# Each gather of edges' rows in the routed experts' attention waits for the landing of the last gather but one

## The chip, the cores and the metric

The kernel runs on one core of a Trainium2 chip. A core has five engines that run their own instruction streams side by side: TensorE (PE, matrix products; PEld is its weight load), VectorE (DVE), ScalarE (ACT), GpSimd (POOL) and SyncE (SP), and 16 DMA engines that move data between main memory (HBM) and on-chip memory (SBUF). Engines wait for each other and for DMA by semaphores. The metric is device time in microseconds (us) from start to end of one execution, as the median over several; a profile is one further execution.

## The reference, cut to what matters

The kernel computes eight blocks, one behind the other, on 3125 nodes of 256 features: a graph layer and a feed-forward layer, four times. The change is in the second block, the feed-forward layer of routed experts, whose router is a small graph attention over 32768 edges:

```python
h = (x_flat @ W_gat).reshape(M, HEADS, NUM_EXPERTS)      # 4 heads, 4 experts
src = jnp.concatenate([edge_index[0], loops])            # 32768 edges and a loop for each node
dst = jnp.concatenate([edge_index[1], loops])
a_src = (h * att_src).sum(-1)
a_dst = (h * att_dst).sum(-1)
e = jax.nn.leaky_relu(a_src[src] + a_dst[dst], negative_slope=0.2)
e_max = jax.ops.segment_max(e, dst, num_segments=M)
ee = jnp.exp(e - e_max[dst])
denom = jax.ops.segment_sum(ee, dst, num_segments=M)
alpha = ee / (denom[dst] + 1e-16)
agg = jax.ops.segment_sum(h[src] * alpha[:, :, None], dst, num_segments=M)
...
topk_s, topk_i = jax.lax.top_k(scores, TOP_K)            # 2 of 4, from agg's layer norm
w = jax.nn.softmax(topk_s, axis=-1)
for ei in range(NUM_EXPERTS):
    g = jnp.where(topk_i == ei, w, 0.0).sum(-1)
    hh = jax.nn.gelu(x @ W1[ei] + b1[ei], approximate=False)
    out = out + g[..., None] * (hh @ W2[ei] + b2[ei])
```

The experts' products do not need the attention; only the last sum, where each expert's output is weighted by its gate, needs both.

## The kernel before, in words

The nodes are padded to 3200 = 25 tiles of 128 (`NT` = 25, `P` = 128). An earlier stage has sorted the edges by their destination; `gsorted` in HBM holds their source nodes in that order, and `gstart_i` says for each node where its edges start. The function of this stage is `routed_layer_in_order` (L1204). It goes as follows.

- The router's logits `hg` and the two sides of the attention's score come from PE and DVE. `node` packs, for each node, 4 scores and 16 logits, which makes a row of 20 numbers or 80 bytes. SP writes it to `nodes` in HBM (L1219).
- The gathers, which are what the change is about: for each of 8 groups, POOL issues 32 indirect DMAs (L1230; the instruction itself is in the helper `gather`, L236), each of which fetches 128 rows of `nodes`, one per partition, into a column of `ge`. Behind each group POOL issues a plain DMA that writes `ge` to the table `edges` in HBM (L1232, 320 KB). There are 256 such gathers in all; `ge` has two buffers. Software-issued DMAs share eight semaphores in turn, and so each gather in the built program waits for the semaphore of the one eight before it.
- `routed_experts` (L1192): for each of 4 experts and each of 7 chunks of columns (six of 512 nodes, one of 128), 8 matrix products `l0f_ph` (L1200), 4 Gelus on ACT (L1201, tile `l0f_ht`), 16 products or fewer of L576 in pairs of loops (tile `l0f_po`, inside the helper `project`), and DVE adds the bias while it empties PSUM (L1288, "evacuation"; 13 of them for each expert). Expert 0's outputs stay in SBUF (`l0f_y_first`), the others go to HBM through `l0f_ys` (L1290).
- The attention itself, in `shares`, is called in the last expert's chunks 2 to 6, each time for five tiles of nodes. POOL gathers from `edges` 40 rows for each node (`el`, five gathers of 128 descriptors of 3200 bytes); DVE copies the node's own row in (L1253), adds the destination's score (L1255), takes the leaky ReLU (L1256), the mask, the maximum and the difference (L1257 to L1259); ACT takes the exponential (L1261); DVE sums (L1262), multiplies (L1264) and adds up the messages (L1269 to L1271). I call these steps for one call the attention chain of a chunk. `tc.issue_after` (L1252, L1260) asks that the first DVE part be ordered behind the chunk's second evacuation, and the exponential behind the chunk's last Gelu.
- `router_gates` (L1114; its first step is L1121, tile `ag`) makes gates from the sums, all on DVE and ACT. Then X is updated with the experts' weighted outputs on DVE (L1302, L1310), and the next stage's normalisation gives `xn` (L456), which PE transposes (L465).

The order of instructions on each engine is set by a planner: it simulates the program with costs that it assumes and lists each engine's instructions by due time. An edit that changes a cost or a dependency can so move instructions elsewhere. `tc.add_manual_dep` adds a dependency between two instructions by hand.

Of the kernel before, what the change touches and what calls it, by code (L numbers as in the profile page):

```python
# [209 lines left out]
def body(ctx, tc, A, out, plan):  # L210
    nc = tc.nc
    V, S, G, T = nc.vector, nc.scalar, nc.gpsimd, nc.tensor

    def pool(stack, name, bufs=1, space=None):
        kw = {} if space is None else {"space": space}
        return stack.enter_context(tc.tile_pool(name=name, bufs=bufs, **kw))
# [6 lines left out]
    def load(stack_pool, ap, shape, name, dtype=F32, **kw):  # L223
        t = stack_pool.tile(shape, dtype, name=name, **kw)
        nc.sync.dma_start(t, ap)
        return t
# [6 lines left out]
        return t  # L233

    def gather(dst, table, idx):
        G.indirect_dma_start(out=dst, out_offset=None, in_=table, in_offset=bass.IndirectOffsetOnAxis(ap=idx, axis=0))  # L236

    def scatter(table, idx, src, **kw):
        G.indirect_dma_start(out=table, out_offset=bass.IndirectOffsetOnAxis(ap=idx, axis=0), in_=src, in_offset=None, **kw)  # L239
# [385 lines left out]
    def edge_softmax(st, nt, chunk, W, dst_row, dst_i, dst_f, sc_i, states, score):  # L625
# [8 lines left out]
        for t in range(nt):  # L634
# [6 lines left out]
            one = slice(t, t + 1)  # L641
            row = ep.tile([P, state.shape[1]], F32, name="row", bufs=6)
            gather(row, state[:NP, :], dst_i[:, one])
            s, v = score(ep, t, row[:, SW:])
            mine = rows[:, k * P : (k + 1) * P]
# [66 lines left out]
    def windows_of(wp, ps, groups, places):  # L712
# [4 lines left out]
        for g in groups:  # L717
            n, K = len(g), WKS[g[0]]
            wd = wd_all[:, g[0] : g[0] + n, :K]
            for t in g:  # L720
                gather(wd_all[:, t, :K].rearrange("p k w -> p (k w)"), plan["rec"][:, :], plan["first"][:, t : t + 1])
# [482 lines left out]
    def routed_layer_in_order():  # L1204

        with ExitStack() as st:
# [5 lines left out]
            with ExitStack() as st2:  # L1212
# [5 lines left out]
                nodes = dram.tile([NP, 20], F32, name="nodes")  # L1218
                nc.sync.dma_start(nodes[:, :].rearrange("(t p) w -> p t w", p=P), node)  # L1219
                part = load(ga, gsorted[:, :].rearrange("(p j) o -> p (j o)", p=P), [P, GT], "src_parts", I32)  # L1220
# [3 lines left out]
                nc.sync.dma_start(edges[GE:, :], pad)  # L1224
                by_part = edges[:GE, :].rearrange("(p j) w -> p j w", p=P)
                gx = pool(st2, "gat_e", 2)
                for j0 in range(0, GT, 32):
                    ge = gx.tile([P, 32, 20], F32, name="ge")
                    for j in range(32):
                        gather(ge[:, j, :], nodes[:, :], part[:, j0 + j : j0 + j + 1])  # L1230

                    G.dma_start(by_part[:, j0 : j0 + 32, :], ge)  # L1232

# [159 lines left out]
    if plan:  # L1393
        routed_layer_in_order()
    else:
        routed_layer_by_states()
# [318 lines left out]
    with ExitStack() as st:  # L1715
# [30 lines left out]
        for e in range(8):  # L1746
# [3 lines left out]
            for c, cl in CHUNKS:  # L1750
                src, at = xt, c
                for layer in range(2):
                    dst = wp.tile([P, 2, 512], F32, name=f"l1f_h{layer}")
# [290 lines left out]
    with ExitStack() as st:  # L2044
# [66 lines left out]
        for i in range(2):  # L2111
            idx = {}
# [125 lines left out]
```

## Time and profile before

| | us |
|---|---|
| median of 6 runs | 5787.35 |
| lowest and highest of them | 5781.7, 5794.35 |
| the profiled execution | 5770.04 |
| its span | 5768.2 |

The mean granted PE clock of the profiled execution is 0.84. Over the span, PE is busy 74%, PEld 46%, DVE 40%, ACT 21%, POOL 27%. The gathers of the change (`ge<-nodes,src_parts`) are 256 instructions of 944 ns on average, 241.7 us in all. The matrix products of this stage are 196.6 us (L1200) and 188.6 us (L576).

In the views, a line of a group reads: line, engine, operation, tile written from tiles read, count, busy time, mean of one, idle time of the engine in front of them and what ended most of it. "remote" is a wait whose releaser the profile does not show. "issue" is time in which the engine waited for nothing that the profile shows. A line of the timeline begins with the start and the duration, both in us, and ends with the idle time before it and its releaser.

### The profile page before, as it was taken

The numbers are of one execution on the slowest core, as the hardware profiler recorded it, in microseconds if no ns is written. First come the engines' busy times: TensorE is split into PE (matmuls) and PEld (weight loads), VectorE is DVE, ScalarE is ACT, GpSimd is POOL, SyncE is SP. The second block draws the span as 40 slices with busy tenths as digits, with TensorE's granted clock in tenths as the row PEclk, the third lists the DMA queues.
The fourth block names the chain that finished last, engine by engine and source line by source line (L and its number), as shares of the span: only waits on it lengthen the run. The fifth ranks groups of instructions, "written<-read, shape, count | busy, mean of one in ns | idle before, by whom it ended". The sixth has DMA issues, their size and how long they took to land. (4 is left out here: it accounts for less than half of the span.)

```text
span 5768.2 us, 56008 instructions
## 1 busy us (share of the span) xinstructions
PE 4263.1 (74%) x20805; PEld 2625.9 (46%) x20889; DVE 2314.3 (40%) x6281; ACT 1186.2 (21%) x2820; POOL 1533.4 (27%) x1496
## 2 busy tenths in 40 slices
PE   2467778215956996666668767788999999797987
PEld 2344444103634664445447433445444445463455
DVE  8765342000075233556555656665101102324042
ACT  0245530001221221333331211222101100120011
POOL 2145440762010002555550356541000000220010
PEclk6667779657978997777878888889999999898999
DMA  1034562001133335554551222210222132224300
GB/s 49 15 127 151 170 202 85 15 14 51 47 128 111 128 128 163 151 153 141 154 151 62 96 92 95 82 50 29 71 77 83 62 96 88 81 81 179 134 24 23
DMA packets 286839, 553.51 MB, mean 96 GB/s; under 512 B 81979, under 2 KB 195148, under 8 KB 275676
## 3 DMA queue, kind: packets, MB, share of 16 engines
q1 hardware_dynamic: 215804, 411.42, 21.1%
q0 software_dynamic: 70752, 138.40, 8.8%
q8 instruction: 167, 2.74, 0.2%
q14 instruction: 116, 0.95, 0.1%
HBM read 377.47 MB, written 172.20 MB: 95 GB/s over the span
## 5 line engine op out<-in xcount | busy, mean ns | idle before, releaser
L558 PE MATMUL agg_ps<-tt,h_l 128*128 128x512 bf16 (+3 forms) x3796 | 882.4, 393 | 54.3 <-ACT h_l L2018 43.8
L236 POOL DMA_INDIRECT h_kv<-kv_tab,kv_row x416 | 435.8, 1048 | 878.9 <-ACT h_odt L1615 562.0
L239 POOL DMA_INDIRECT wgt_cells<-cw_wsum,cw_to x391 | 386.4, 988 | 346.7 <-DVE cw_to L1108 201.0
L558 PEld LDWEIGHTS <-h_l 128*128 128x128 bf16 x3150 | 291.2, 98 | 330.9 <-issue 15.6
L239 POOL DMA_INDIRECT gsorted<-gs_i,gpos x256 | 304.2, 1188 | 434.4 <-DVE gpos L909 321.0
L1200 PE MATMUL l0f_ph<-xt,l0f_w 128*128 128x512 f32 (+1 forms) x448 | 196.6, 583 | 257.0 <-issue 162.4
L1628 PE MATMUL h_pq<-h_q,h_odt 128*128 128x256 bf16 x1248 | 224.4, 351 | 133.3 <-DVE h_qk L1630 100.0
L236 POOL DMA_INDIRECT ge<-nodes,src_parts x256 | 241.7, 944 | 253.7 <-PE l0f_po L576 160.2
L1757 PE MATMUL l1f_ph<-l1f_h,l1f_W 128*128 128x512 f32 (+1 forms) x448 | 226.1, 637 | 96.8 <-ACT l1f_h L1760 83.4
L1760 ACT ACTIVATE l1f_h<-l1f_ph,bn_shift,bn_scale 128x512 f32<-128x512 f32 (+1 forms) x224 | 162.4, 731 | 629.4 <-PE l1f_ph L1757 322.1
L576 PE MATMUL l1f_po<-l1f_Wo,l1f_h 128*128 128x256 f32 x800 | 225.7, 415 | 79.2 <-issue 34.8
L1815 DVE TENSOR_TENSOR at<-agg_ps,rdeg_r 128x512 f32<-128x512 f32 (+1 forms) x42 | 25.6, 633 | 586.3 <-PE agg_ps L558 586.3
L1628 PEld LDWEIGHTS <-h_odt 128*128 128x128 bf16 x1248 | 150.9, 125 | 224.9 <-issue 178.4
L1935 POOL IOTA trash_slot<- 128x32 f32 x1 | 0.2, 158 | 948.2 <-PE l2g_ph L1834 948.2
L1200 PEld LDWEIGHTS l0f_ph<-xt,l0f_w 128*128 128x128 f32 x448 | 84.4, 199 | 352.6 <-issue 248.7
L576 PEld LDWEIGHTS l1f_po<-l1f_Wo,l1f_h 128*128 128x128 f32 x800 | 155.4, 203 | 176.5 <-issue 78.2
L1681 PE MATMUL h_po<-h_kv,h_of 128*128 128x256 f32 x832 | 217.7, 427 | 21.4 <-DVE h_kv L1677 21.4
L576 PE MATMUL l0f_po<-l0f_w,l0f_ht 128*128 128x256 f32 x800 | 188.6, 393 | 39.1 <-ACT l0f_ht L1201 22.3
L558 PEld LDWEIGHTS agg_ps<-tt,h_l 128*128 128x128 f32 x700 | 126.3, 192 | 189.3 <-issue 188.6
L1757 PE MATMUL l1f_ph<-xt,l1f_W 128*128 128x512 f32 (+1 forms) x448 | 207.1, 586 | 1.1 <-issue 1.1
L1681 PEld LDWEIGHTS h_po<-h_kv,h_of 128*128 128x128 f32 x832 | 179.8, 219 | 52.5 <-DVE h_kv L1677 22.6
L465 PE MATMUL pt<-ident,xn 128*128 128x128 f32 x300 | 64.7, 376 | 180.4 <-DVE xn L456 135.5
(625 smaller groups left out, 7575.0 us busy)
## 6 DMA issues: line engine op xcount, KB each, us to landing
tt<-cnt_ds SPq DMA_DIRECT2D x90, 640.0 KB
kv_tab<-kv SPq DMA_DIRECT2D x50, 1024.0 KB
tt<-wgt_cells SPq DMA_DIRECT2D x30, 1280.0 KB
wgt_cells<-cw_zero SPq DMA_DIRECT2D x6, 5800.0 KB
cw_row<-cell_r SPq DMA_DIRECT2D x23, 1128.0 KB
cw_ew<-in_ew_r_dram SPq DMA_DIRECT2D x22, 1108.0 KB
cnt_ds<-row_ds SPq DMA_DIRECT2D x150, 128.0 KB
cnt_sd<-cols SPq DMA_DIRECT2D x6, 3200.0 KB
```

The costliest lines, as they stand in the source:

```text
L236: G.indirect_dma_start(out=dst, out_offset=None, in_=table, in_offset=bass.IndirectOffsetOnAxis(ap=idx, axis=0))
L239: G.indirect_dma_start(out=table, out_offset=bass.IndirectOffsetOnAxis(ap=idx, axis=0), in_=src, in_offset=None, **kw)
L465: T.transpose(pt[:, j, :], src[:, g + j, h * P : (h + 1) * P], ident)
L558: T.matmul(acc[h][:, :width], part[:, s, h * P : (h + 1) * P], tt[:, s - s0, :width], start=(s == 0 and i == 0), stop=(s == NT - 1 and i = ...
L576: T.matmul(psum, lhs[:, i, t * P : (t + 1) * P], rhs[:, i, :], start=(i == 0), stop=(bias is None and i == k - 1))
L1200: T.matmul(ph[:, :cl], w1[:, k, f * P : (f + 1) * P], xt[:, k, c : c + cl], start=(k == 0), stop=(k == 1))
L1628: T.matmul(pq[:, i, :], odt[:, k0 + i, :], q3[:, j, :], start=(j == 0), stop=(j == 2))
L1681: T.matmul(po, of[:, j, :], kv[:, j, D:], start=(k0 + j == 0), stop=(k0 + j == K - 1))
L1757: T.matmul(ph[:, :cl], ws[layer][:, k, o * P : (o + 1) * P], src[:, k, at : at + cl], start=(k == 0), stop=(k == 1))
L1760: S.activation(dst[:, o, :cl], ph[:, :cl], AF.Relu, bias=shi[:, col], scale=sca[:, col])
L1815: V.tensor_tensor(at[:, hf, c : c + cl], psum, rdeg_r[:, c : c + cl], op=OP.mult)
L1935: G.iota(trash, pattern=[[P, 32]], base=NP, channel_multiplier=1, allow_small_or_imprecise_dtypes=True)
```

## The change

`gather` returns its instruction. The loop over the 256 gathers collects them, and each one from the third on gets a dependency on the gather two before it, so that it waits on that gather's semaphore, that is until its 128 rows have landed.

```diff
     def gather(dst, table, idx):
-        G.indirect_dma_start(out=dst, out_offset=None, in_=table, in_offset=bass.IndirectOffsetOnAxis(ap=idx, axis=0))
+        return G.indirect_dma_start(out=dst, out_offset=None, in_=table, in_offset=bass.IndirectOffsetOnAxis(ap=idx, axis=0))
...
                 gx = pool(st2, "gat_e", 2)
+                got = []
                 for j0 in range(0, GT, 32):
                     ge = gx.tile([P, 32, 20], F32, name="ge")
                     for j in range(32):
-                        gather(ge[:, j, :], nodes[:, :], part[:, j0 + j : j0 + j + 1])
+                        got.append(gather(ge[:, j, :], nodes[:, :], part[:, j0 + j : j0 + j + 1]).ins)
+
+                        if len(got) > 2:
+                            tc.add_manual_dep(
+                                got[-1], got[-3].name, mybir.DependencyInfo(mybir.DependencyClass.Sync, mybir.DependencyReason.DATA), reason="rows landed"
+                            )
 
                     G.dma_start(by_part[:, j0 : j0 + 32, :], ge)
```

Lines behind the edges write have numbers six higher in the changed file than before.

## The prediction

> **What bounds the kernel now.** The chain that ended last covers only the end of the program (from 4061 us on) and does not reach this stage, so the place of the change is read from busy time by stretch of the stage, then from the waits in it, then from POOL's own instructions.
>
> Busy time in seven stretches (start:end, length, then PE, PEld, DVE, ACT, POOL busy with counts, granted clock, DMA share, GB/s):
>
> ```profile
> 860.00:1000.00 140.00, 119.44 (x574) 62.39 (x580) 41.84 (x130) 11.53 (x20) 0.23 (x1) 0.93 0.32 94
> 1000.00:1150.00 150.00, 46.33 (x129) 27.01 (x127) 2.77 (x4) 5.50 (x8) 113.97 (x122) 0.63 0.10 15
> 1150.00:1344.00 194.00, 24.07 (x48) 12.05 (x48) 2.77 (x4) 2.75 (x4) 132.17 (x142) 0.54 0.09 16
> 1344.00:1500.00 156.00, 136.40 (x474) 90.83 (x475) 13.04 (x20) 27.67 (x44) 9.45 (x10) 0.90 0.18 63
> 1500.00:1614.00 114.00, 113.93 (x409) 76.33 (x408) 11.45 (x18) 23.45 (x36) 0.00 (x0) 1.00 0.10 39
> 1614.00:1661.00 47.00, 45.00 (x167) 30.02 (x166) 44.53 (x41) 19.85 (x25) 10.68 (x10) 1.00 0.37 121
> 1661.00:1774.00 113.00, 0.27 (x2) 0.22 (x2) 103.50 (x236) 7.64 (x9) 4.75 (x5) 0.52 0.49 163
> ```
>
> While POOL issues the 256 gathers (999.8 to 1338.4) nothing else is busy: PE 70 us of 344, ACT 8, DVE 6, DMA engines 10%. Afterwards PE is full (113.93 of 114) with the other experts, and from 1661 to 1774 it stands still behind DVE. Expert 0 takes 990.5 to 1399, some 407 us; experts 1 to 3 take 262 together, 87.2 each. The waits between 990 and 1700 (engine, line, releaser: us, times, longest):
>
> ```profile
> ACT l0f_ht L1201 <- remote: 331.2, 10, 100.2
> POOL el L236 <- DVE gat_num L1271: 299.2, 3, 278.1
> DVE l0f_y_first L1288 <- issue: 195.1, 4, 88.9
> PE l0f_ph L1200 <- issue: 162.4, 14, 76.8
> ```
>
> The expert loop reads nothing of a gather: its waits in the program are on PE, ACT and DVE. Yet a Gelu waits up to 100 us with no releaser on the page, and its releases lie 10 to 11 us apart or multiples of that. I call this the clog. It begins some 12 gathers after the first and ends by 1373, about 17 us after the last of the ten `el` gathers that follow. POOL in the same time, forms and then its last steps:
>
> ```profile
> L236 POOL DMA_INDIRECT ge<-nodes,src_parts x256: 938/944/988, 999.8 to 1338.4; - x128
> L1232 POOL DMA_DIRECT2D edges<-ge x8: 578/591/604, 1044.5 to 1341.3; - x8
> ```
> ```profile
> 1338.41 0.94 POOL L236 DMA_INDIRECT ge<-nodes,src_parts  x1 [1.16 <-issue]
> 1341.31 0.58 POOL L1232 DMA_DIRECT2D edges<-ge  x1 [1.95 <-DMA ge<-nodes,src_parts]
> 1344.03 0.97 POOL L236 DMA_INDIRECT el<-edges,gstart_i  x1 [2.15 <-DMA edges<-ge]
> ```
>
> A gather is 0.944 us with 0.30 behind it: 1.25 from start to start as far as about 1214, 1.40 after that, 338.6/255 = 1.33 on average. The recorded landings are 2.0 to 2.45 us after a gather's start, all the way.
>
> How the stage ends:
>
> ```profile
> 1613.59 0.69 DVE L1288 TENSOR_TENSOR l0f_ys<-l0f_po,l0f_b 128x512 f32<-128x512 f32 x1 [2.76 <-PE l0f_po L576]
> 1614.48 1.01 DVE L1255 TENSOR_TENSOR gat_s<-el,side_L_ffn_att_dst 128x820 f32<-128x820 f32 x1
> 1700.09 0.58 DVE L1121 TENSOR_TENSOR ag<-gat_num,den 128x400 f32<-128x400 f32 x1
> 1773.73 2.10 PE L465 MATMUL pt<-ident,xn 128*128 128x128 f32 x8 [112.98 <-DVE xn L456]
> ```
>
> The attention chain starts right behind evacuation 6 of expert 3 (1613.59), ends with the gates' first step at 1700.09, and PE's next stage waits for DVE until 1773.73. So the stage is gathers, then experts, then DVE's chain.
>
> **The change part by part.**
>
> *The waits.* Gather n waits for the landing of n-2 in place of n-8 (254 of the 256 get the wait). No instruction is added. Two starts lie 2.50 us apart; the landing is there after 2.0 to 2.45, and POOL starts some 0.25 after a landing (edges landed 2.47 after 1341.31, `el` started at 1344.03). That makes 2.25 to 2.70 for two gathers: 1.25 (the floor of 0.944 + 0.30) to 1.35 each. The dearest row is the last gather to its edges write, 1341.31 - 1338.41 = 2.90: 1.45 each. Against 1.33 now: 255 x (1.45 - 1.33) = +31 at most, 255 x (1.25 - 1.33) = -20 at least. I take +8, near 1.36: the landings are the nearest row, the 2.90 is of the clogged end.
>
> Under "Anatomy of one DMA — SWDGE (gpsimd) path", the Trainium skill's page "DMA: Bandwidth & Descriptors" puts a transfer at 2.0 us plus bytes over 436e3: an estimate of 2.02 for 10 KB. By it the wait never binds and this term is nothing; the row of 2.90 would make it +31.
>
> *What queues behind the waits.* On POOL the eight edges writes, then `el`. The first edges write comes after 33 gathers in the built program (36 before), so it waits for a gather just issued: 2.90 - 1.33 = 1.6 us for each of eight, 13 at most, inside the bounds above. `el` is next needed when the chain starts, and POOL has nothing else until 2236. If experts and gathers keep their pace, `el` has about 270 us of slack (1344 to 1614). Its cover goes only at 1.33 + 270/255 = 2.4 us per gather. Later gathers cost time only because the clog lasts as long as they do: then one to one.
>
> *The order.* The planner counts the gathers as later and moves the chain. Built, DVE runs ten evacuations of expert 3 ahead of the first L1255, not six; ACT's first Exp stands behind all 24 large Gelus. Two chunks of 13.77 us: the chain starts at 1614.48 + 27.5 = about 1642. Gained back: four evacuations that lay inside it are ahead of it (4 x 0.69 = 2.8). Lost: the first Exp waits for the 24th Gelu and its table load (about 1648.7 + 1.28 + 0.89 = 1650.9, against 1647.5 for DVE's own steps, +3.4); fewer waits for ACT later, some -2. Sum +26 at L1121, 1726 for 1700. All of it counts: PE already waits 113 us behind DVE, everything behind is in the old order, and the loads for the next stage are released with L1121 and have their own idle time (DMA 49%). Before, the experts' matmuls hid this chain's beginning; from 1661 on nothing does. SP's order is unchanged.
>
> *Sum if the clog stays:* +26 + 8 = +34, with bounds +6 and +57 from the gathers. On the profiled execution, 5770.0 becomes 5804; that execution is 17.3 us under the median of the runs, so on 5787.35 it is 5821.
>
> **The rivals.**
>
> *The waits dissolve the clog (faster).* For it: the clog is tied to uninterrupted gathers. In a later stage a burst of gathers at 1.25 behaves alike: tiny matmuls run freely and then, twelve gathers in, stand 1.2 to 1.3 us apart:
>
> ```profile
> 2287.89 1.16 PE L1655 MATMUL h_pm<-h_top,h_odt 128*128 128x4 bf16 x38 [2.10 <-issue]
> 2290.27 0.16 PE L1655 MATMUL h_pm<-h_top,h_odt 128*128 128x4 bf16 x1 [1.22 <-issue]
> 2291.71 0.16 PE L1655 MATMUL h_pm<-h_top,h_odt 128*128 128x4 bf16 x1 [1.28 <-issue]
> ```
>
> There pauses of 7 to 9 us end it. POOL's own 1.40 after 1214 looks like the rate that can be sustained; a wait that holds gathers above it would keep the way clear. Then experts 0 to 3 run 87.2 us each, to 990.5 + 348.8 = 1339; gathers end between 1328 (1.25) and 1379 (1.45 and the edges writes), `el` is ready 13 later, and the chain, 82 us alone, reaches L1121 between 1423 and 1474 in place of 1700: -226 to -277, 5510 to 5561. Against it: that needs 1.40, and the landings allow 1.25 to 1.35; in the clog no more than two gathers are on their way as it is, so the wait changes hardly anything there.
>
> The Trainium skill speaks against this rival too: "SBUF — State Buffer", "Who interferes with whom", says that "PE and ACT never wait on anyone". The row of 331.2 us on ACT disagrees, and by the page the gain of this rival would be nothing.
>
> *Partly (faster).* At 1.33 to 1.38 the clog forms later or breaks at some edges writes. If a quarter to a half of the 250 us is regained, 63 to 125 less the 34: -30 to -90, 5700 to 5757. For it: the rates allowed lie just under 1.40. Against: POOL's own 1.40 from 1214 did not break it.
>
> *No visible change.* The order's 26 is just met by a clog that begins some gathers later: 5776 to 5799. It needs a gain of 15 to 38 us by chance. That the change does not do what it says, with every wait already met, is in the first case: the order alone still costs +26, 5813.
>
> **How the numbers follow.** A measurement of this kernel tells 0.2%, 11.6 us, from no change. Chances: clog stays 0.53, all of it slower; dissolved 0.27; partly 0.15; no visible change 0.05. So slower 0.53, same 0.05, faster 0.42. The time is the likeliest case's, 5821; its own range is 5800 to 5850 (the bounds and the runs' spread of some 6 us). For eight in ten it must take in most of the dissolved case: 5530 to 5855, leaving out about 0.1 below and 0.05 above.
>
> **What would show it.** Right: ACT at L1201 still waits some 330 us for a releaser that is not shown, expert 0 ends near 1400, gathers start 1.3 to 1.4 us apart, L1261 of the changed file (L1255 here) first runs near 1642, the gates' first step near 1726 to 1735. Wrong: ACT's Gelus 13.8 us per chunk while gathers run, expert 3 done before 1400 and the granted clock near 1.0 between 1000 and 1344 (dissolved), or gathers over 1.45 us apart, with the experts' restart after 1410 (a dearer wait than any row shows).

## The result, and the profile after

The changed kernel takes 5804.31 us (median of 33 runs) beside 5781.06 us (median of 72 runs of the kernel before): ratio 1.0038, 95% interval 1.0029 to 1.0047, which is 17 to 27 us more. The prediction said slower, 5821 on 5787, a ratio of 1.006; the time lies inside its range of 5800 to 5850.

The profiled execution has a span of 5803.5 us, 35.3 more than that of before. Of these, 15.6 us lie in front of the point where PE begins the next stage (1789.4, before 1773.7). Counted from the first gather, which comes 1.9 us earlier in the changed kernel (997.9, before 999.8), they are 17.5. The other 19.7 lie behind it, 19.2 of them in the feed-forward layer of the second pair, from the start of its first matrix product to that of its last activation (3232.8 to 4043.7, before 3216.4 to 4008.1). The instructions there are the same in the same order. The two other kernels below that were profiled under the same conditions, unchanged there, need 3969 and 3991 us behind this point, before and after 3994.5 and 4014.1, and that layer alone takes 780.8 to 810.9 us in the four profiles: so this part is put down to scatter between executions, and a single pair of profiles must be read by stage. The 15.6 us are the part to explain.

Busy time in the stretch in which POOL gathers, before and then after (columns: start:end, length, PE, PEld, DVE, ACT, POOL busy with counts, granted clock, DMA share, GB/s):

```profile
1000.00:1344.00 344.00, 70.41 (x177) 39.07 (x175) 5.53 (x8) 8.24 (x12) 246.14 (x264) 0.58 0.10 15
```
```profile
1000.00:1344.00 344.00, 89.69 (x216) 49.11 (x214) 6.13 (x9) 11.00 (x16) 245.18 (x263) 0.60 0.09 15
```

The stall of the other engines is still there, but PE does 19 us more work in it. Two of the waits of the changed kernel from 990 to 1740, the gathers, the evacuations of experts 1 to 3 (before, then after), and how the attention begins and ends:

```profile
ACT l0f_ht L1201 <- remote: 322.4, 9, 100.2
...
POOL ge L236 <- DMA ge<-nodes,src_parts: 19.9, 53, 1.4
```
```profile
L236 POOL DMA_INDIRECT ge<-nodes,src_parts x256: 941/946/992, 997.9 to 1339.4; - x128
```
```profile
L1288 DVE TENSOR_TENSOR l0f_ys<-l0f_po,l0f_b x39: 412/691/693, 1409.6 to 1669.7; 128x512 f32<-128x512 f32 x36, 128x256 f32<-128x256 f32 x3
```
```profile
L1294 DVE TENSOR_TENSOR l0f_ys<-l0f_po,l0f_b x39: 408/692/693, 1399.2 to 1656.1; 128x512 f32<-128x512 f32 x36, 128x256 f32<-128x256 f32 x3
```
```profile
1630.68 0.69 DVE L1294 TENSOR_TENSOR l0f_ys<-l0f_po,l0f_b 128x512 f32<-128x512 f32 x1 [2.76 <-PE l0f_po L576]
1631.29 1.00 DVE L1261 TENSOR_TENSOR gat_s<-el,side_L_ffn_att_dst 128x820 f32<-128x820 f32 x1
...
1640.46 1.63 DVE L1268 TENSOR_REDUCE gat_den<-gat_s 128x20 f32<-128x820 f32 x1 [3.38 <-ACT gat_s L1267]
...
1716.29 0.57 DVE L1121 TENSOR_TENSOR ag<-gat_num,den 128x400 f32<-128x400 f32 x1
1789.38 2.10 PE L465 MATMUL pt<-ident,xn 128*128 128x128 f32 x8 [139.84 <-DVE xn L456]
```

The new wait is seen as 53 stops of POOL for a landing, 19.9 us in all. The gathers are 341.5/255 = 1.34 us apart (before 1.33): they take 2.9 us longer and, begun 1.9 us earlier, end 1.0 us later. The chain starts behind evacuation 10 (1630.68), two chunks later in the order, and 16.8 us later in time, not 27.5, since the experts themselves are earlier: expert 1's first evacuation starts at 1399.2 (before 1409.6), their last product at 1649.2 (before 1660.4). The 3.38 us in front of L1268 are the wait for the first exponential that the prediction put at 3.4. The gates' first step is at 1716.3, 16.2 later than before.

### The profile page after: what moved, and what is told of

It is laid out like the page before. It is cut to its first block, busy times and chain, and to the rows that moved or that the text cites. A ratio compares the mean times of both kernels' runs of the same rounds, so it can differ in the third digit from the quotient of the medians.

```text
span 5803.5 us, 55992 instructions
## 1 busy us (share of the span) xinstructions
PE 4261.3 (73%) x20805; PEld 2622.3 (45%) x20889; DVE 2315.3 (40%) x6281; ACT 1181.2 (20%) x2816; POOL 1538.0 (27%) x1496
```

## The experiments

The chips differ. On two of them, and in the runs of the result, the kernel before takes 5735 to 5787 us and the engines stall while gathers run. On three others it takes 4975 to 4977 us and there is no stall. Each of the five chips was met in one sitting, so it is not known whether the chip or the moment makes the difference; for short, the text speaks of chips with and without the stall. Each experiment is compared with the kernel before on its own chip, and the text says which kind it met.

**The two halves of the change, each alone.** `order_only` keeps the gathers as before and puts the attention by hand into the changed order, or nearly: the first chain stands behind evacuation 10 as there, but the first exponential behind 23 of the large Gelus, not 24:

```diff
+                    mults.append(mult.ins)      # mult: the product of L1264
...
-                    k = c // 512 - 2
-                    if e == 3 and k >= 0:
-                        shares(5 * k, put.ins, last.ins)
+                    if e == 3 and c // 512 == 4:
+                        shares(0, put.ins, last.ins)
+                        shares(5, mults[-1], last.ins)      # behind L1264 of the chunk before
+                    if e == 3 and c // 512 == 6:
+                        for k in (2, 3, 4):
+                            shares(5 * k, mults[-1], last.ins)
```

> The kernel before, with its own waits on the gathers, but with the attention chains put by hand into the order of the changed kernel (first chain behind evacuation 10 of the last expert, exponentials behind the 24 large Gelus). Theory A (the loss is the order's): expert 0's outputs still start to be stored near 1410 as before, experts end near 1658, the chain starts near 1641, the gates' first step comes 22 to 28 us later than the 1700 of before, and the ratio is 1.004 to 1.005. Rival B (the loss is the waits' own): gates' first step within 3 us of 1700, ratio 1.000.

`waits_old_order` is the changed kernel with ordering edges that hold DVE and ACT in the order of before:

```diff
+                        marks["max", d0 // 5] = ...      # and "sub", "exp" and "mult" likewise
...
+                        if e == 3 and j == 0:    # evacuations behind steps of the attention
+                            behind(put.ins, {3: ("mult", 0), 4: ("sub", 1), 5: ("sub", 2), 6: ("max", 3)}.get(c // 512))
...
+                    if e == 3 and behind is not None:    # Gelus behind exponentials
+                        behind(last.ins, {(3, 3): ("exp", 0), (4, 0): ("exp", 0), (5, 0): ("exp", 1), (6, 0): ("exp", 2)}.get((c // 512, f)))
```

> The changed kernel with its waits on the gathers, but with the attention chains held in the order of before (first chain behind evacuation 6, exponentials between the Gelus). Theory A: the waits thin the gathers to 1.29 us and let expert 0 end some 10 us earlier, nothing else; the gates' first step near 1690, 8 to 12 us earlier than before, ratio 0.998. Rival B: gates' first step near 1716 as in the changed kernel, ratio 1.003 to 1.004.

Both met a chip without the stall, for which neither expectation was written; the ratio of 1.000 that rival B gave `order_only` came, for another reason. `order_only`: 4977.24 us on 4977.42, ratio 0.9995 (0.9986 to 1.0004). `waits_old_order`: 5015.09, ratio 1.0078 (1.0064 to 1.0092). There the waits cost 38 us and the order nothing, the reverse of theory A. The two halves have not been run with the stall. To see why, both kernels of the case were profiled on such a chip.

> The kernel before, for a profile of it under the conditions of the first four runs, in which PE stayed busy while the gathers ran and the whole took about 4977 us. If those conditions hold: gathers 1.25 us apart from about 840 to 1162, PE busy 98% or more from 840 to 1160, the gates' first step within 5 us of 1265, time near 4977. If the conditions of the first profiles hold (PE, ACT and DVE nearly still while gathers run): gates' first step near 1700, time near 5780.

> The changed kernel, beside the one before. If PE stays busy while the gathers run: the waits cost what they cost with the old order, the last gather 38 to 42 us later than before, the gates' first step later by as much, ratio 1.007 to 1.009 (rival: with the changed order too the two losses add up, 60 us and more). If PE stands still while they run: ratio 1.003 to 1.005.

`before_again`: 4976.8 us, ratio 0.9997 (0.9987 to 1.0008). `after_again`: 5014.61, ratio 1.0075 (1.0059 to 1.0092). Busy time in two stretches of `before_again` (columns as above), then the timeline where DVE first uses the attention's rows, then the forms of the gathers and of the gates' first step (duration in ns, then first and last start):

```profile
840.00:1000.00 160.00, 159.93 (x576) 107.91 (x575) 16.34 (x24) 32.38 (x49) 120.31 (x129) 1.00 0.16 39
1000.00:1160.00 160.00, 144.11 (x521) 96.32 (x519) 14.16 (x22) 31.01 (x48) 121.59 (x131) 0.96 0.21 59
```
```profile
1179.56 1.01 DVE L1255 TENSOR_TENSOR gat_s<-el,side_L_ffn_att_dst 128x820 f32<-128x820 f32 x1 [44.73 <-DMA el<-edges,gstart_i]
```
```profile
L236 POOL DMA_INDIRECT ge<-nodes,src_parts x256: 940/944/991, 841.6 to 1164.3; - x128
...
L1121 DVE TENSOR_TENSOR ag<-gat_num,den x1: 574/574/574, 1266.9 to 1266.9; 128x400 f32<-128x400 f32 x1
```

The same of `after_again`, with POOL's wait for landings (total us, times, longest) in place of the busy time:

```profile
POOL ge L236 <- DMA ge<-nodes,src_parts: 89.1, 183, 2.5
```
```profile
1220.95 1.01 DVE L1261 TENSOR_TENSOR gat_s<-el,side_L_ffn_att_dst 128x820 f32<-128x820 f32 x1 [57.95 <-DMA el<-edges,gstart_i]
```
```profile
L236 POOL DMA_INDIRECT ge<-nodes,src_parts x256: 938/942/988, 842.3 to 1205.6; - x128
...
L1121 DVE TENSOR_TENSOR ag<-gat_num,den x1: 576/576/576, 1303.6 to 1303.6; 128x400 f32<-128x400 f32 x1
```

From 840 to 1000 PE is busy all the time (159.93 of 160 us, granted clock 1.00) beside 129 of POOL's DMAs. Expert 3's first chunks are done before the edges' table is, and DVE waits 44.73 us for `el`. So the gathers are the bound here. The last one comes 41.3 us later in the changed kernel, L1255 (L1261) 41.4 later, the gates' first step 36.7 later (its chain is 5 us shorter, with more evacuations ahead of it), the whole 38. The order has no say, because `el` comes after evacuation 10 in any case.

The distance is 363.3/255 = 1.425 us, near the upper end of the prediction's bounds (1.45). All 16 semaphore increments of nearly every gather are recorded on these chips, where the first profiles had only some of them. The last increment comes 2.30 us after a gather's start in the median, and 2.83 or more in one of ten. Half of (2.30 + 0.25) is 1.28, and the median distance is 1.25 to 1.30 in each group of 32. Against 1.25 that is 255 x 0.03 = 8 us of the 41. Most of the rest is the tail: within the groups of 32, 29 distances are over 1.6 us and hold 28 us above 1.28. In the changed kernel with the stall only 6 are, with 7 us. That the experts' own transfers make the tail (DMA share 0.15 to 0.20 here, 0.09 with the stall) is likely and was not tried.

**Other depths**, still on chips without the stall. `n3` is the changed kernel with `len(got) > 3` and `got[-4]`, and with the ordering edge from each gather to the next that `every4_kept` shows below; its attention stands in the order of before. `n1_all` is the changed kernel with `len(got) > 1` and `got[-2]`.

> Each gather waits for the landing of the one three before it, 3.75 us earlier at 1.25 us each. If PE stays busy: only landings later than 3.5 us bind, distance 1.25 to 1.27, ratio 0.999 to 1.001 and the order of the attention has no say. If the rival is right that any wait of POOL on a landing costs an issue delay by itself, distance 1.30 or more and ratio 1.003 or more.

> Each gather waits for the landing of the one just before it. Gathers 2.3 to 2.9 us apart, the last at 1590 to 1740. If the stall of PE, ACT and DVE is tied to the rate of the gathers (theory C): Gelus every 13.8 us per chunk from the start, expert 0 in 90 to 110 us, all experts done by 1350 to 1400 while gathers still run, the gates' first step 85 to 100 us after the last gather, near 1760, the whole some 50 to 70 us slower than before. If it is tied to gathers being under way at all (rival D): expert 0 lasts until the gathers end, experts until 1900 to 2000, 200 to 300 us slower.

`n3`: 4982.42 us, ratio 1.0011 (1.0002 to 1.0021), distance 1.288, gates' first step 1273.5, 6.6 later. It lies between the two expectations: a depth of three still meets the tail of late landings (one in ten later than 2.97 us, some beyond 4), but most of the cost is gone. `n1_all`: 5334.14, ratio 1.0716 (1.0696 to 1.0736), distance 2.69, last gather 1524.4, gates' first step 1622.5. All its experts are done at 1176. It says nothing of the stall, which this chip does not have, but shows gathers as the bare bound: 98 us behind the last gather the gates begin, 103 in `before_again`.

`every4` lets only each fourth gather wait, for the one just before it:

```diff
-                        if len(got) > 2:
+                        if len(got) % 4 == 0:
                             tc.add_manual_dep(
-                                got[-1], got[-3].name, ...
+                                got[-1], got[-2].name, ...
```

> Only every fourth gather waits, for the one just before it; the order of the attention is that of before. Mean distance (3 x 1.25 + 2.6) / 4 = 1.59, last gather near 1406. Theory C, with a sustainable distance of about 1.40: no stall, expert 0 in 90 to 110 us, all experts done by 1400, the gates' first step near 1500 to 1510, 190 to 200 us faster, ratio 0.965 to 0.97. Rival D: expert 0 until about 1440, the gates' first step near 1765, ratio 1.011.

It took 4976.66 us, ratio 0.9998 (0.9988 to 1.0007), distance 1.27, and tested nothing: the planner had put other gathers between the two, so that each landing was there in time. `every4_kept` holds the gathers in their written order with an ordering edge from each to the next; every other engine has the order of before.

```diff
+                        if len(got) > 1:
+                            tc.add_manual_dep(
+                                got[-1], got[-2].name, mybir.DependencyInfo(mybir.DependencyClass.NoSync, mybir.DependencyReason.DATA), reason="in order"
+                            )
```

> Every fourth gather waits for the one just before it, and the gathers are held in their written order (in every4 the planner had sent other gathers in between, so that the waits were met). Mean distance (3 x 1.25 + 2.69) / 4 = 1.61, 92 us more for 256 gathers. If PE stays busy while the gathers run: the gathers are the last to end, gates' first step 85 to 95 us later, ratio 1.018. If PE stands still while they run: theory C (a mean distance above 1.40 frees it) says experts done by 1420 and 180 to 200 us faster; rival D says some 60 to 90 us slower.

5067.18 us, ratio 1.0183 (1.0162 to 1.0203), distance 1.632, gates' first step 1357.5, 90.6 later: as expected without the stall.

**The order where `el` is early.** To give the attention its rows early without a stall, `half_old_order` gathers only every second group and writes each group's rows to the table twice. `half_new_order` is the same on `order_only`.

```diff
-                    ge = gx.tile([P, 32, 20], F32, name="ge")
-                    for j in range(32):
-                        gather(...)
+                    if j0 % 64 == 0:
+                        ge = gx.tile([P, 32, 20], F32, name="ge")
+                        for j in range(32):
+                            gather(...)
```

> The kernel before with only every second group of gathers (128 of 256; each group's rows are written to the edges' table twice, so half of the edges carry other rows), the attention in the order of before. If PE stays busy while gathers run: the rows for the attention are there near 1010, long before the experts need them, so the chain starts behind evacuation 6 of the last expert at about 1136 and the gates' first step comes near 1222, 45 us earlier than in the kernel before. If PE stands still while they run: the stall is about half as long and the chain starts as now behind evacuation 6.

> The same with 128 gathers, with the attention in the changed kernel's order (the order_only edit). Theory A, the prediction's own working of the order: the chain starts two chunks later, near 1164, and the gates' first step comes 22 to 28 us after that of half_old_order, 0.45 to 0.55% of the time. Rival (the order costs nothing, as with 256 gathers under these conditions): within 5 us of it.

4928.83 us, ratio 0.9907 (0.9891 to 0.9924), and 4952.79 us, ratio 0.9953 (0.9936 to 0.9969), on one chip without the stall: 24 us apart. The timeline where the chain begins, and the forms of the gathers and of the gates' first step, of the old order and then of the new:

```profile
1135.51 1.01 DVE L1256 TENSOR_TENSOR gat_s<-el,side_L_ffn_att_dst 128x820 f32<-128x820 f32 x1
```
```profile
L236 POOL DMA_INDIRECT ge<-nodes,src_parts x128: 940/944/1012, 842.3 to 1004.6; - x128
...
L1121 DVE TENSOR_TENSOR ag<-gat_num,den x1: 575/575/575, 1221.1 to 1221.1; 128x400 f32<-128x400 f32 x1
```
```profile
1160.20 1.01 DVE L1258 TENSOR_TENSOR gat_s<-el,side_L_ffn_att_dst 128x820 f32<-128x820 f32 x1
```
```profile
L236 POOL DMA_INDIRECT ge<-nodes,src_parts x128: 940/944/1011, 839.2 to 1001.5; - x128
...
L1121 DVE TENSOR_TENSOR ag<-gat_num,den x1: 574/574/574, 1243.9 to 1243.9; 128x400 f32<-128x400 f32 x1
```

From the first gather to the gates it is 1221.1 - 842.3 = 378.8 us and 1243.9 - 839.2 = 404.7: the order costs 25.9 us when `el` is early, close to the prediction's +26. (The first wait for an exponential is 1.4 us here, where the changed kernel has 3.4.) With 256 gathers and no stall it is 425.3 in `before_again` and 1263.1 - 839.5 = 423.6 in `order_only`: nothing.

**With the stall.** `half_waits` is `half_old_order` with the changed kernel's waits and the edges of `waits_old_order`.

> half_old_order (128 gathers, attention in the order of before) with the changed kernel's wait on each gather. If the waits cost only by making the attention's rows late: gathers 1.40 to 1.45 us apart instead of 1.27, the last 15 to 25 us later than in half_old_order, but still 100 us before the rows are needed; the chain starts behind evacuation 6 near 1136, the gates' first step near 1221, ratio as half_old_order's, 0.990 to 0.992. Rival (a waiting POOL slows other engines or their transfers as well): the gates' first step 10 us later or more, ratio 0.993 or more.

It met a chip with the stall: 5579.51 us beside 5734.89 of the kernel before, ratio 0.9712 (0.9668 to 0.9756). Its own question, whether the waits cost anything but the lateness of `el`, is not answered, since the half without waits was not run there. It shows something else:

```profile
1000.00:1180.00 180.00, 67.57 (x190) 40.14 (x188) 4.84 (x7) 9.62 (x14) 125.67 (x136) 0.67 0.10 21
```
```profile
L236 POOL DMA_INDIRECT ge<-nodes,src_parts x128: 938/944/1007, 1003.6 to 1174.9; - x128
...
L1121 DVE TENSOR_TENSOR ag<-gat_num,den x1: 574/574/574, 1529.1 to 1529.1; 128x400 f32<-128x400 f32 x1
```

The last gather is 163.5 us earlier than in the first profile of before, and the gates' first step 171.0. As far as two profiles from different chips show it, the stall lasts about as long as the gathers do, as the prediction had it.

`every4_kept_2` is `every4_kept` once more, to find the other kind of chip.

> The same kernel as every4_kept (every fourth gather waits for the one just before it, mean distance about 1.6), once more, for the condition of the first profiles and of half_waits, in which PE, ACT and DVE nearly stand still while gathers run. In that condition theory C (above a mean distance of some 1.40 nothing stalls) says expert 0 ends by 1110, all experts by 1400, last gather near 1410, gates' first step near 1500 to 1520, ratio 0.965 to 0.972; rival D (gathers stall the engines whatever their distance) says expert 0 ends near 1470, gates' first step 60 to 90 us later than before, ratio 1.010 to 1.016. If it meets the other condition it repeats every4_kept, ratio 1.018.

It did: 5596.83 us beside 5772.47, ratio 0.9699 (0.9665 to 0.9733). Busy time while it gathers, two of its waits, the gathers and the gates' first step, POOL around one stop, and last a wait of the second pair's feed-forward layer in the same profile:

```profile
1012.00:1344.00 332.00, 302.59 (x1088) 202.70 (x1086) 30.50 (x46) 62.74 (x96) 194.50 (x208) 0.96 0.16 44
```
```profile
ACT l0f_ht L1201 <- PE l0f_ph L1200: 211.5, 89, 8.6
...
POOL ge L236 <- DMA ge<-nodes,src_parts: 110.6, 66, 3.2
```
```profile
L236 POOL DMA_INDIRECT ge<-nodes,src_parts x256: 942/947/992, 1012.0 to 1428.7; - x128
...
L1121 DVE TENSOR_TENSOR ag<-gat_num,den x1: 574/574/574, 1532.4 to 1532.4; 128x400 f32<-128x400 f32 x1
```
```profile
1051.54 0.94 POOL L236 DMA_INDIRECT ge<-nodes,src_parts  x1 [0.30 <-issue]
1052.79 0.95 POOL L236 DMA_INDIRECT ge<-nodes,src_parts  x1 [0.30 <-issue]
1054.04 0.95 POOL L236 DMA_INDIRECT ge<-nodes,src_parts  x1 [0.30 <-issue]
1056.53 0.95 POOL L236 DMA_INDIRECT ge<-nodes,src_parts  x1 [1.54 <-DMA ge<-nodes,src_parts]
```
```profile
ACT l1f_h L1770 <- remote: 146.6, 16, 30.3
```

Three gathers at 1.25 us and one stop behind them, 1.634 us on average, and in this stage the stall is gone: PE is busy 302.59 of 332 us where it was 70.41 of 344, no Gelu waits for a hidden releaser, expert 1's first evacuation starts 98 us after expert 0's first product (in the first profile of before 419, in `every4_kept` without the stall 98). The condition itself had not gone: in the later layer, whose instructions are unchanged, ACT still waits 146.6 us for hidden releasers (207.5 in the first profile of before, none in `before_again`). The gathers now take 417 us where they took 339, and still the gates' first step comes 520 us after the first gather, not 700. From the first gather to PE's next stage it is 594 us, in `every4_kept` 593, in the first profile of before 774.

So rival D, that gathers stall the engines whatever their distance, is out. Theory C gave the ratio rightly; its "experts done by 1400" was missed, since the last products (to 1492.9) stand behind the attention, which waits 139 us for `el`. Its rule, a mean distance above some 1.40, is not shown: 1.34 and 1.63 were tried, and what frees the engines may as well be the stop for a landing after every fourth gather as the mean distance.

## Why the prediction was right

*Place and cover: right.* The stall stays, DVE's chain sets the end of the stage, and the difference at L1121 (+16.2) comes through to PE (+15.6).

*The order, +26: right in size.* The chain behind evacuation 10, the Exp behind 24 Gelus with 3.38 us of waiting, and 25.9 us in the pair of half-kernels that changes only this. In the profiled pair it is 16.2 at L1121 plus the 10.5 by which expert 1's first evacuation comes earlier (1399.2, before 1409.6), 27. That sum is worked out; the order alone was not run with the stall.

*The gathers, +8: too high, and in the profiled pair wrong in sign.* The sentence that this pair contradicts is "Later gathers cost time only because the clog lasts as long as they do: then one to one." The distance was well placed (1.34; 1.36 was taken), and the gathers took 2.9 us longer. But from the first gather to expert 1's first evacuation it is 401.3 us, before 409.8: 8.5 less, at a point where the two orders do not differ yet (with the 1.9 us by which the gathers begin earlier, 10.5). The stall is not all or nothing: PE did 19 us more work in the same stretch. With -10.5 for +8 the prediction's own sum gives +15.5, the profiled pair's 16. In the medians, which moved by 17 to 27 us, an order of 27 leaves -10 to 0 for the gathers, where +8 was taken.

That the waits bring this gain is not shown. It rests on one profile of each kernel, and the layer of the second pair, which has the same kind of waits, varies by 30 us between profiles without any change. `half_waits` points the same way (expert 1's first evacuation 63.6 us behind the last gather, 59.8 in the changed kernel, 71.2 before). One reason could be that the waits spread the gathers: they lie 1.27 to 1.30 us apart in the median of each group, where before it was 1.25 in the first six groups and 1.40 in the last two. Then how the gathers are spread counts as well as when they end. `waits_old_order`, which was meant to show the gain alone, met a chip without the stall.

*The rival "dissolved": possible, and not met.* It asked for a distance above 1.40 and the landings did not give one. At 1.34 the stall stays; at 1.63, with a stop after every fourth gather, it is gone. Where between these it ends, and whether distance or stop ends it, was not tried. The rival's share, 0.27, was for an effect that exists: with that pattern of waits it was worth 176 us (5596.83 beside 5772.47).

*What the prediction could not see* is that its profile belonged to one kind of chip. Without the stall the change is slower too, by 0.75%, but by the other term: the waits' own lateness, with a distance of 1.425 near the dearest row (1.45), and no cost of the order. The recorded landings of 2.0 to 2.45 missed the tail, because few of a gather's 16 increments were recorded, of most gathers one or two.

*Two slips in its numbers* change nothing: expert 0 took 408.5 us by the bounds that it gives, not 407, and its lower bound of +6 makes 5793, not the 5800 of its own range.

## What to carry to other kernels

A wait that limits how many gathers are under way is sized by the last of a gather's increments and by their tail, not by the median: at a depth of two the median allowed 1.28 us and the tail made it 1.43 on chips without the stall. An edit that makes a planner believe that a transfer is later moves the consumers too, and this can cost more than the wait; hold the order by hand, or look at each engine's order before the time. And where several engines stall while one issues many small DMAs, their pace is worth trying by itself: here a stop after every fourth gather was worth 3% on a chip that stalls and cost 1.8% on one that doesn't. The changed kernel and this one are the only versions that were run on both kinds, and neither is faster on both.

## What the runs showed of the hardware

The same kernel took 4975 to 4977 us on three chips and 5735 to 5787 in the other runs, with the same instructions. On the former, PE is busy 159.93 of 160 us beside 129 of POOL's DMAs; on the latter 70 of 344. The stall depends on how POOL's gathers are spaced (there at 1.34 us, gone at 1.63 with a stop after every fourth). More than this stage is slower: of the 793 us between the first profile of before and `before_again`, 158 lie ahead of the first gather, 276 from there to PE's next stage, 117 from there to the second pair's feed-forward layer, and 242 in that layer (791.7 us, 550.0 in `before_again`); behind it the two need the same 1760 us. In each of these four stretches POOL issues hundreds of indirect DMAs (`gsorted` 256, `ge` 256, `h_kv` 416, `wgt_cells` 391); that these cause all of the 793 us was not tried.

With the stall the trace also lacks most of the gathers' semaphore increments: in the first profile all 16 are recorded for none of the 256 gathers, in `before_again` for 255. Where the stall is gone from this stage, in `every4_kept_2`, it is 132. What carries the stall, whether the recording itself takes part, and why some chips have it, is open.

The Trainium skill says in "SBUF — State Buffer", "Who interferes with whom", that PE and ACT never wait on anyone. That section is about the engines' ports to SBUF. What ACT waits for here, up to 100 us, is a semaphore whose release the trace does not show, so these profiles neither confirm the sentence nor contradict it, and the prediction read it too widely. PE's 159.93 of 160 us without the stall agree with it.
